# A gated graph layer on one Trainium2 core: table and result stores on ScalarE's queue, table copies on SyncE's

## The chip, the cores and the metric

The kernel runs on one core of a Trainium2 chip. Its time is the device time of a whole execution in microseconds (us). It is given as the median over several runs. A profiled execution is a run of its own: the profile's times are made against that run and not against the median.

The engines are TensorE (PE, matrix products; PEld is its weight load), VectorE (DVE), ScalarE (ACT), GpSimd (POOL) and SyncE (SP). SyncE computes nothing here: it only issues DMA transfers. ScalarE and GpSimd issue transfers as well, between their other instructions. A DMA that SyncE issues goes by queue q1, one that ScalarE issues by q10, and the gathers of GpSimd by q0. Each engine goes through its instructions in a fixed order.

## The reference

Sixteen batches of 1024 nodes with 256 values each, one adjacency matrix for all of them. About 0.8% of its entries, and its diagonal, are not zero.

```python
pre_u = einsum('bud,dk->buk', h, W1[:d])
pre_v = einsum('bvd,dk->bvk', h, W1[d:])
hidden = relu(pre_u[:, :, None, :] + pre_v[:, None, :, :] + b1)
S = sigmoid(einsum('buvk,ko->buvo', hidden, W2)[..., 0] + b2[0])
a = einsum('buv,bud->bvd', S * A, h)
m = einsum('uv,bud->bvd', A, h) * h
z = beta1 * h + beta2 * (a @ Wa + ba) + beta3 * (m @ Wm + bm)
```

So each target node v sums its neighbours' rows h_u twice: once scaled by the entry of A and a gate S of the edge, and once by the entry of A alone. The kernel computes the gate only for the edges that are there.

## The kernel before

**Tables.** The batches form 4 groups of 4. For each group g there is a table in HBM with one row of 8 KB per node: the first half holds pre_u of the four batches, the second half a copy of h of the four batches. A gather of 128 rows thus brings all that 128 edges need.

**Blocks and steps.** The loop runs over 32 blocks, each with one group and 128 targets. Targets 0 to 5 of groups 0 and 1 come first, then their targets 6 and 7, then groups 2 and 3. A block has 2 windows of 5 slots, so 10 steps of 128 edges, and there are 320 steps. In a step

- GpSimd gathers 128 table rows into one of 8 buffers (line 518),
- TensorE spreads pre_v of the targets over the edges (615) and VectorE adds it to the rows (647),
- VectorE takes relu times W2 and sums, four times, one for each batch (655),
- ScalarE takes the sigmoid (658) and scales the edges' one-hot columns by the gate (660, with 625 for the part without a gate),
- TensorE sums the rows of the slot into the targets (672).

At the end of a window half, ScalarE copies the sums out (680), TensorE transposes them (690), ScalarE copies those (693), and VectorE multiplies the m part by h (704). At the end of a block TensorE multiplies by Wa and Wm (721), ScalarE copies the product (726), and VectorE adds beta1 times h in the block's buffer h_blk (727).

**Work beside it.** Group 0's table is made ahead of the loop. The rows of the others are made inside it, piece by piece, where a script written out by hand puts them. For 128 nodes of a group: load_hT (434) brings the transposed h by SyncE; copy_h (439) copies h straight from the input in HBM into the table's second half; half_product (445) makes pre_u for two batches at a time; ScalarE copies it into one of two buffers, tab0 and tab1 (461), each of which exists once; and a store brings that to the table (465). Line 467 is the same store for rows made ahead of the loop, where one buffer holds all four batches.

h_blk has four buffers. It is loaded from the table at steps 5 and 7 of each block by SyncE (911) and stored to the output two steps after its product (729). The last block has its own load (917) and its own stores (767), shared by SyncE and ScalarE.

**What sets the order.** All of this is issued in a fixed order for each engine. `after(step, f)` puts a small action on a list for a later step, and `do(n)` runs the list of step n after that step's gate. The store of a tab buffer is put one step after its copy, and the store of h_blk two steps after its product. A DMA instruction whose data or buffer isn't ready holds everything behind it on the engine that issues it.

Of the kernel before, what the change touches and what calls it, by code (L numbers as in the profile page):

```python
# [13 lines left out]
P = 128  # L14
# [3 lines left out]
def kernel(  # L18
# [42 lines left out]
    nc = tc.nc  # L61
# [22 lines left out]
    table = [dram.tile([N, 2 * GD], FP, name=f"table{g}") for g in range(NG)]  # L84
# [135 lines left out]
    def small(name):  # L220
        return psm.tile([P, 512], FP, name="misc")
# [180 lines left out]
    def after(step, f):  # L402
        due.setdefault(step, []).append(f)
# [19 lines left out]
    def drop_hT(k):  # L423
        del hTs[k]
        if k in hT_of:
            hT_free.append(hT_of.pop(k))
# [7 lines left out]
        engine.dma_start(hTs[k].rearrange("p b c n -> p (b c) n"),  # L434
                         xT_rows[:, g * GB * DC:(g + 1) * GB * DC, nt * P:(nt + 1) * P])

    def copy_h(k, engine=nc.scalar):
        g, nt = k
        engine.dma_start(table[g][nt * P:(nt + 1) * P, GD:].rearrange("n (b d) -> n b d", b=GB),
                            x_rows[nt * P:(nt + 1) * P, g * GB:(g + 1) * GB, :])  # L440

    def half_product(p, hT, wt, h, begun):
        for bb in range(2):
            for i in range(DC):
                nc.tensor.matmul(p[:, bb * D:(bb + 1) * D], hT[:, 2 * h + bb, i, :], wt[:, i, :],  # L445
                                 start=(i == 0 and not begun), stop=(i == DC - 1), skip_group_check=begun)

    def add_row(p, parts):
        nc.tensor.matmul(p, unit, parts.unsqueeze(1).to_broadcast([P, 2, D]),  # L449
                         start=True, stop=False, skip_group_check=True)  # L450

    def rows(k, tab=None):

        g, nt = k
        for h in range(2):
            step = yield
            c = slice(2 * h * D, (2 * h + 2) * D)
            p = small("p")
            half_product(p, hTs[k], w_u, h, False)
            t = big.tile([P, 2 * D], FP, name=f"tab{h}", bufs=1) if tab is None else tab[:, c]  # L460
            nc.scalar.copy(t, p)
            if h == 1 and k in again:
                drop_hT(k)
            if tab is None:
                after(step + 1, lambda t=t, c=c: nc.sync.dma_start(table[g][nt * P:(nt + 1) * P, c], t))
        if tab is not None:
            after(step + 1, lambda: nc.sync.dma_start(table[g][nt * P:(nt + 1) * P, :GD], tab))

# [72 lines left out]
    for i in range(COPIES):  # L541
        copy_h(turn[i], nc.sync)
# [17 lines left out]
    for t, turns_ in enumerate(script):  # L560
        step = t - 100
        do(step)
        for c in turns_.split():
            if c == "r":
                if m % 2 == 0:
                    piece = rows(turn[m // 2], tabs[m // 2] if m // 2 < len(tabs) else None)
                    next(piece)
                go(piece, step)
                if m % 2 == 0 and m // 2 + COPIES < NT:
                    copy_h(turn[m // 2 + COPIES], nc.sync)  # L570
# [138 lines left out]
    def block_end(k):  # L709

        g, vt = order[k]
        hb = hbs[k]
        for h in range(2):
            for i, wt in ((1, w_a), (0, w_m)):
                step = yield
                if i:
                    pz = small("pz")
                    add_row(pz, bias_p)
                for bb in range(2):
                    for c in range(DC):  # L720
                        nc.tensor.matmul(pz[:, bb * D:(bb + 1) * D], LTs[k][:, 2 * h + bb, i if bb else 1 - i, c, :], wt[:, c, :],  # L721
                                         start=False, stop=(i == 0 and c == DC - 1), skip_group_check=True)
            z = pz.rearrange("p (b d) -> p b d", b=2)
            if step >= ROOM:
                z = LTs[k][:, 2 * h].rearrange("p k c n -> p (k c n)").rearrange("p (b d) -> p b d", b=2)
                nc.scalar.copy(z, pz.rearrange("p (b d) -> p b d", b=2))
            after(step + 1, lambda hb=hb[h], z=z: nc.vector.scalar_tensor_tensor(hb, hb, be1, z, ALU.mult, ALU.add))  # L727
            b = g * GB + 2 * h
            after(step + 2, lambda hb=hb[h], b=b: nc.sync.dma_start(
                out[b:b + 2, vt * P:(vt + 1) * P, :].rearrange("b p d -> p b d"), hb))  # L730
        del hbs[k], LTs[k]

# [59 lines left out]
    def made_rows(n):  # L792
        nonlocal piece, last
        if n in loads and loads[n] in turn[NT:NT + 2] and loads[n] not in begun:
            copy_h(loads[n])
            begun.add(loads[n])
        elif n in loads:
            if loads[n] in begun and loads[n][0] == 1:
                aside_.remove(loads[n])
            load_hT(loads[n])  # L800
            if loads[n] not in begun:
                copy_h(loads[n])
                begun.add(loads[n])
        if n in at:
            if at[n] != last:
                last = at[n]
                piece = rows(last)
                next(piece)
            go(piece, n)

    def products(n, k, s):
# [5 lines left out]
        if z <= s < z + 4 and 0 < k < BS:  # L817
            if s == z:
                end = block_end(k - 1)
                next(end)  # L820
            go(end, n)
# [50 lines left out]
    for n in range(total + 2):  # L872
        k, s = divmod(n, T)
# [32 lines left out]
        if s in (5, 7) and k < BS - 1:  # L906
            h = s // 7
            hb = big.tile([P, 2, D], FP, name="h_blk", bufs=4)
            hbs.setdefault(k, []).append(hb)
            g, vt = order[k]  # L910
# [31 lines left out]
    with tc.If(any_left > 0):  # L942
        with ExitStack() as s2:
# [4 lines left out]
            for vt in range(NT):  # L948
                hb = fb.tile([P, B, D], FP, name="fb_h")
# [100 lines left out]
```

## Time and profile before

| what | value |
|---|---|
| three runs | 1085.15, 1085.4, 1089.84 us; median 1085.4 |
| profiled execution, own time | 1098.79 us |
| its span in the profile | 1097.0 us |
| mean granted TensorE clock | 0.984 of full speed |
| GpSimd's gathers, line 518 | 320; q0 has 70.4% of the DMA time |
| q1 (SyncE) | 83776 packets, 78.66 MB, 22.5% of the DMA time |
| q10 (ScalarE) | 13296 packets, 13.11 MB, 3.5% |
| all DMA | 394.56 MB at a mean of 360 GB/s |
| DMAs issued in the loop by SyncE | h_blk loads 62, result stores 62, tab stores 48 |
| DMAs issued in the loop by ScalarE | copies of h 24 |

How to read it: a line such as "L465 SPq" names the kernel's line and the engine; the letter q after an engine means the engine's own issuing of DMAs and not its computing. "Busy" of an engine counts only its computing instructions. A wait "A <- B" says that A stood idle until B was done. A "remote" releaser is one that the profile could not name. The chain of waits is followed back from the last instruction. A row of slices gives, for a stretch of the span, how long each engine was busy in it.

### The profile page before, as it was taken

To read this page: it belongs to the slowest core of one execution; us is meant where nothing else is said; L and a number is where in the kernel's file an instruction comes from. 1 tells how busy PE (TensorE), PEld (TensorE's weight loads), DVE (VectorE), ACT (ScalarE), POOL (GpSimd) and SP (SyncE) were. 2 spreads that over 40 slices of the span, in tenths; PEclk is the share of its full clock that TensorE was granted. 3 is DMA by queue.
4 is the path that set the end of the run, shared out by engine and by line. 5 is a ranking of instruction groups with operands and counts; after the bars stand their busy time and mean duration, and the time that the engine had idled before them with its cause. 6 is when DMAs were issued, how large, how long until landed. Compare 5 with 4: busy or idle time off the path is not lost.

```text
span 1097.0 us, 24059 instructions
## 1 busy us (share of the span) xinstructions
PE 1027.7 (94%) x7645; PEld 730.7 (67%) x7645; DVE 1022.9 (93%) x3487; ACT 862.6 (79%) x2616; POOL 456.9 (42%) x456
## 2 busy tenths in 40 slices
PE   7777898999999999999999999999999999999986
PEld 6654676676666776667766777777766666666653
DVE  8686999898999999999998999999999999999994
ACT  3246787778888887798878888898889888888973
POOL 2665675455347334553332342333333333333330
PEclk9888999999999999999999999999999999999999
DMA  9989999999999999999999999999999999999991
GB/s 289 317 332 373 323 329 366 316 377 375 401 361 376 398 403 370 373 384 394 400 392 349 410 390 392 399 391 397 369 366 363 373 349 355 362 373 356 357 343 44
DMA packets 147752, 394.56 MB, mean 360 GB/s; under 512 B 18224, under 2 KB 94512, under 8 KB 111408
## 3 DMA queue, kind: packets, MB, share of 16 engines
q0 software_dynamic: 50544, 301.16, 70.4%
q1 hardware_dynamic: 83776, 78.66, 22.5%
q10 hardware_dynamic: 13296, 13.11, 3.5%
q8 instruction: 63, 1.03, 0.4%
q14 instruction: 73, 0.60, 0.1%
HBM read 396.93 MB, written 50.33 MB: 408 GB/s over the span
## 4 chain that ended last, share of the span: by engine, by line
PE 53%; DVE 26%; DMA 8%; issue 7%; ACT 4%; SPq 1%; POOL 1%; another core or an unknown queue 0%; ACTq 0%; POOLq 0%; DVEq 0%
PE misc L445 14%; PE acc L672 13%; DVE fetched L655 12%; PE misc L721 11%; DVE fetched L647 10%; PE pc L615 9%; PE misc L690 3%; DMA fetched<-table,uidx 2%; DMA table<-tab 2%; DMA out_dram<-h_blk 2%; PE misc L449 2%; DVE low L484 1%; ACT left L660 1%; DVE LT L704 1%; DVE h_blk L727 1%
## 5 line engine op out<-in xcount | busy, mean ns | idle before, releaser
L518 POOL DMA_INDIRECT fetched<-table,uidx x320 | 338.0, 1056 | 548.4 <-PE acc L672 412.9
L655 DVE SCALAR_TENSOR_TENSOR fetched<-fetched,w_b 128x256 f32<-128x256 f32 x1280 | 478.3, 420 | 0.0
L647 DVE TENSOR_TENSOR fetched<-fetched,pc 128x1024 f32<-128x1024 f32 x320 | 387.8, 1212 | 39.4 <-PE pc L615 25.9
L660 ACT ACTIVATE left<-left,gt 128x32 f32<-128x32 f32 (+1 forms) x1280 | 299.6, 305 | 10.4
L672 PE MATMUL acc<-fetched,left 128*32 128x256 f32 x4096 | 281.6, 385 | 12.0 <-issue 4.6
L615 PE MATMUL pc<-X,mark 128*128 128x512 f32 x640 | 244.7, 464 | 15.2 <-DVE fetched L647 14.8
L672 PEld LDWEIGHTS acc<-fetched,left 128*32 128x32 f32 x4096 | 128.7, 109 | 125.0 <-issue 38.0
L615 PEld LDWEIGHTS pc<-X,mark 128*128 128x128 f32 x640 | 106.0, 190 | 93.6 <-issue 40.4
L658 ACT ACTIVATE gt<-sc,b_b 128x4 f32<-128x4 f32 x320 | 95.9, 300 | 45.3 <-DVE fetched L655 40.1
L721 PE MATMUL misc<-w_m,LT 128*128 128x256 f32 x496 | 117.3, 379 | 0.0
L721 PE MATMUL misc<-w_a,LT 128*128 128x256 f32 x496 | 117.2, 379 | 0.0
L445 PE MATMUL misc<-w_v,hT 128*128 128x256 f32 x448 | 108.4, 386 | 0.0
L721 PEld LDWEIGHTS misc<-w_a,LT 128*128 128x128 f32 x496 | 93.8, 189 | 15.3 <-issue 0.4
L721 PEld LDWEIGHTS misc<-w_m,LT 128*128 128x128 f32 x496 | 93.8, 190 | 15.1
L625 ACT ACTIVATE left<-onehot,val 128x64 f32<-128x64 bf16 (+1 forms) x320 | 102.9, 322 | 0.0
L655 DVE DVE_READ_ACCUMULATOR fetched<-fetched,w_b 128x1 f32 x1280 | 101.0, 79 | 0.0
L385 POOL DMA_INDIRECT val<-in_adjT_dram,vidx x80 | 86.3, 1079 | 34.3 <-issue 20.7
L445 PEld LDWEIGHTS misc<-w_v,hT 128*128 128x128 f32 x448 | 87.0, 194 | 14.4
L690 PE MATMUL misc<-ident,ev 128*128 128x128 f32 x512 | 80.6, 281 | 17.1 <-ACT ev L680 6.1
L690 PEld LDWEIGHTS misc<-ident,ev 128*128 128x128 f32 x512 | 60.9, 142 | 45.5 <-ACT ev L680 16.2
L482 ACT CAST X<-misc 128x512 fp32r<-128x512 f32 x64 | 37.1, 579 | 59.3 <-PE misc L445 44.9
L693 ACT COPY LT<-misc 128x512 f32<-128x512 f32 x128 | 72.9, 570 | 11.9 <-PE misc L690 9.1
(181 smaller groups left out, 1011.4 us busy)
## 6 DMA issues: line engine op xcount, KB each, us to landing
h_blk<-table SPq DMA_DIRECT2D x62, 256.0 KB
out_dram<-h_blk SPq DMA_DIRECT2D x62, 256.0 KB
hT<-in_xT_dram SPq DMA_DIRECT2D x28, 512.0 KB
table<-in_x_dram ACTq DMA_DIRECT2D x24, 512.0 KB
table<-tab SPq DMA_DIRECT2D x48, 256.0 KB
fetched<-table,uidx POOLq DMA_INDIRECT x320
table<-in_x_dram SPq DMA_DIRECT2D x8, 512.0 KB
table<-fetched SPq DMA_DIRECT2D x8, 512.0 KB
```

Source lines behind the costliest of these rows:

```text
L385: nc.gpsimd.indirect_dma_start(out=val[:, i, j:j + 1], out_offset=None, in_=adj_flat, in_offset=bass.IndirectOffsetOnAxis(ap=vidx[:, i, j: ...
L445: nc.tensor.matmul(p[:, bb * D:(bb + 1) * D], hT[:, 2 * h + bb, i, :], wt[:, i, :], start=(i == 0 and not begun), stop=(i == DC - 1), skip ...
L518: nc.gpsimd.indirect_dma_start(out=fetched[at_slot[n]], out_offset=None, in_=table[g], in_offset=bass.IndirectOffsetOnAxis(ap=uidx[:, vt * ...
L615: nc.tensor.matmul(pcs[n][:, c], marks[n // TW][:, j * P:(j + 1) * P], cuts[k][:, w, c], start=True, stop=True)
L625: nc.scalar.activation(lefts[n][:, :m, 1::GB, :], onehot[:, i, o:o + m, :].unsqueeze(2).to_broadcast([P, m, GB // 2, V]), AF.Copy, scale=v ...
L647: nc.vector.tensor_tensor(t, t, pcs.pop(n), ALU.add)
L655: nc.vector.scalar_tensor_tensor(t[:, b, :], t[:, b, :], 0.0, w2_b, ALU.max, ALU.mult, accum_out=sc[:, b:b + 1])
L658: nc.scalar.activation(gt, sc, AF.Sigmoid, bias=b2_b)
L660: nc.scalar.activation(lefts[n][:, :m, 2 * b, :], lefts[n][:, :m, 1 + b // 2 * GB, :], AF.Copy, scale=gt[:, b:b + 1])
L672: nc.tensor.matmul(accs[h][b * 2 * V:(b + 1) * 2 * V, r, :], left[:, i, 2 * b - b % 2:2 * b - b % 2 + 2].rearrange("p k v -> p (k v)"), f[ ...
L690: nc.tensor.transpose(pt[:, r, :, c, :], ev[:, r, c * P:(c + 1) * P], ident)
L721: nc.tensor.matmul(pz[:, bb * D:(bb + 1) * D], LTs[k][:, 2 * h + bb, i if bb else 1 - i, c, :], wt[:, c, :], start=False, stop=(i == 0 and ...
```

## The change

Three calls change their engine; nothing else does.

```diff
-    def copy_h(k, engine=nc.scalar):
+    def copy_h(k, engine=nc.sync):
         g, nt = k
         engine.dma_start(table[g][nt * P:(nt + 1) * P, GD:].rearrange("n (b d) -> n b d", b=GB),
                             x_rows[nt * P:(nt + 1) * P, g * GB:(g + 1) * GB, :])
...
             if tab is None:
-                after(step + 1, lambda t=t, c=c: nc.sync.dma_start(table[g][nt * P:(nt + 1) * P, c], t))
+                after(step + 1, lambda t=t, c=c: nc.scalar.dma_start(table[g][nt * P:(nt + 1) * P, c], t))
...
-            after(step + 2, lambda hb=hb[h], b=b: nc.sync.dma_start(
+            after(step + 2, lambda hb=hb[h], b=b: nc.scalar.dma_start(
                 out[b:b + 2, vt * P:(vt + 1) * P, :].rearrange("b p d -> p b d"), hb))
```

In the loop the 48 tab stores and the 62 result stores are issued by ScalarE instead of SyncE, and the 24 copies of h by SyncE instead of ScalarE. The stores of line 467, the copies ahead of the loop and the last block's own loads and stores stay where they were. The computing instructions of TensorE, VectorE and GpSimd keep their order. ScalarE's list has 1820 rows instead of 1734, which is 110 stores more and 24 copies fewer.

## The prediction

> **What bounds the kernel now.** I read the page from the top: busy shares, the chain that ended last, then the middle of the run in slices of 30 us, then the waits.
>
> ```profile
> PE 1027.7 (94%) x7645; PEld 730.7 (67%) x7645; DVE 1022.9 (93%) x3487; ACT 862.6 (79%) x2616; POOL 456.9 (42%) x456
> ...
> PE 53%; DVE 26%; DMA 8%; issue 7%; ACT 4%; SPq 1%; POOL 1%; another core or an unknown queue 0%; ACTq 0%; POOLq 0%; DVEq 0%
> ```
>
> The first line is busy time, the second the chain. TensorE and VectorE share the bound; ScalarE has 1097.0 − 862.6 = 234 us to spare, 0.73 us in each of the 320 steps. Who bounds where is seen in the slices:
>
> ```profile
> core 0: us, PE busy (x) PEld busy (x) DVE busy (x) ACT busy (x) POOL busy (x), PEclk, DMA share, GB/s
> 510.00:540.00 30.00, 29.93 (x233) 21.78 (x232) 28.76 (x98) 26.20 (x81) 10.49 (x10) 1.00 1.02 396
> 570.00:600.00 30.00, 25.77 (x197) 18.20 (x196) 23.98 (x78) 21.02 (x70) 8.84 (x8) 0.94 0.97 353
> ...
> 180.00:210.00 30.00, 24.50 (x166) 17.06 (x165) 24.01 (x87) 17.83 (x56) 15.81 (x15) 0.94 0.96 319
> ...
> 150.00:180.00 30.00, 29.65 (x226) 21.96 (x219) 29.96 (x104) 25.79 (x80) 18.89 (x20) 1.00 1.02 383
> 900.00:930.00 30.00, 28.79 (x223) 19.99 (x222) 30.00 (x103) 26.84 (x81) 11.25 (x11) 1.00 0.96 355
> 90.00:120.00 30.00, 22.98 (x133) 14.87 (x135) 21.73 (x74) 17.00 (x54) 20.53 (x20) 0.89 0.99 360
> ```
>
> In the middle (510) TensorE never rests; late (900) VectorE never rests. Three slices stand out, in which both rest: 90, 180 and 570. Only such holes can be won by a change that touches queues, unless it makes new ones. What they wait for:
>
> ```profile
> ACT tab L461 <- remote: 10.6, 2, 7.8
> ACT tab L461 <- DMA table<-tab: 5.0, 1, 5.0
> PE misc L690 <- ACT tab L461: 4.4, 2, 3.7
> SPq L729 <- DVE h_blk L727: 418.8, 41, 23.0
> SPq L911 <- DMA out_dram<-h_blk: 21.7, 4, 13.7
> ```
>
> The columns are the total wait, how often, and the longest. ScalarE's copy into the table buffer (line 461) waits three times, at 104, 184 and 577 us. The 577 wait is explained in the SyncE queue's timeline:
>
> ```profile
> 540.48 13.77 SPq L911 DMA_DIRECT2D h_blk<-table  x1
> 554.34 0.40 SPq L729 DMA_DIRECT2D out_dram<-h_blk  x1
> 554.95 5.91 SPq L465 DMA_DIRECT2D table<-tab  x2
> ...
> 565.61 12.33 SPq L729 DMA_DIRECT2D out_dram<-h_blk  x1
> ```
>
> Start and duration lead each line. The buffers were filled by 552, but the stores (465) left only at 554.95, behind a load (911) that held SyncE for 13.77 us; the chain runs through this store for 21.77 us. The next block's copy at 576.80 stood 5.01 us for it, and TensorE's transposes (690) 3.74 us for the copy.
>
> **What the Trainium skill says.** "DMA: Bandwidth & Descriptors", section "Issuing engines are not separate DMA queues": whichever engine starts them, transfers run on the same 16 DMA engines, and several issuers save only sequencer time. The trace agrees as far as it goes: the DMA share is near 1.0 at 360 GB/s whatever queue is busy. Same page, "Queues, rings and completion order": each queue has a ring per DMA engine, served in turn by packet, so a store on the other queue needn't wait behind SyncE's packets. Landings here and below are the last packet of a DMA on its queue in the trace, counted from the issue. Stores not behind an hT load (1024 packets) landed about 4 us after issue (104.92 to 108.9), the mean of tab stores is 7.3 and the worst 16.6 us. "Perfetto Trace Analysis", section "DMA Instruction — HWDGE (DVE, Sync)": an issue's reported time includes waiting for the shared descriptor generator, but not the data movement. The trace fits: 0.33 to 0.56 us normally, up to 13.77 when held.
>
> **The change, part by part.**
>
> *1. The stores leave SyncE.* SyncE loses 48 tab stores and 62 result stores, and with them the waits for VectorE's line 727 (418.8 us of 41 waits). Its other DMAs (hT at 434, h_blk at 911) issue as soon as their buffers are free. The 577 stall is caused by a store kept behind a load; on ScalarE's queue it leaves within a step or two of its copy, more than 20 us ahead of the next. Worth: 29.93 − 25.77 = 4.2 us of TensorE. At 184 the copy waited 2.85 us while SyncE's tab store, issued about 180.3, had stood behind a result store: taken at 2.9 us. Together 7.1 us. Next late there is TensorE itself, as at 510. At 104 SyncE's store was issued at its usual time and other engines waited "remote" too; I take nothing for that one.
>
> *2. ScalarE issues them.* Added: 48 × 0.333 + 62 × 0.388 = 40.0 us of sequencer time; removed: the copies of h, 24 × 0.56 = 13.4; net 26.6 us and 86 instructions. The copies show what such an issue costs ScalarE now. The four scalings (660) with a copy inside and without:
>
> ```profile
> 499.71 0.91 ACT L660 ACTIVATE left<-left,gt 128x16 f32<-128x16 f32 x4
> ...
> 503.34 0.31 ACT L660 ACTIVATE left<-left,gt 128x16 f32<-128x16 f32 x1
> 503.43 0.56 ACTq L439 DMA_DIRECT2D table<-in_x_dram  x1
> 503.55 0.69 ACT L660 ACTIVATE left<-left,gt 128x16 f32<-128x16 f32 x3
> ```
>
> From 503.34 to 504.24 is 0.90 us, against 0.91: the issue ran beside work already queued. Bounds: 0 if always hidden, 26.6 if never; I take 0.6, since 234 us of idle time absorb most of what isn't hidden, and ScalarE is on 4% of the chain.
>
> *3. ScalarE's stores wait, and ScalarE with them.* Behind a waiting store stand the sigmoid (658), the gate scalings, the transposes' copies (693), and for these TensorE. Three kinds:
> - For their data. The tab copy is ScalarE's own. For a result store VectorE's 727 stands in its order ahead of the sums (655) whose sigmoid ScalarE has already used. Nothing new.
> - For a completion semaphore. In the program's listing each DMA of the two queues takes one of eight in turn, and first waits until the DMA eight before has landed. 116 of ScalarE's DMAs wait so, 51 of them for one of SyncE's. Setting the issue times of the new order against the landings of before (hT mean 15.5, worst 39.0 us; h_blk 10.3 and 23.3), about a dozen have under 3 us in hand, and four have landed too late in the loop, by 4.8, 3.1, 1.1 and 1.0: 10 us in all. ScalarE's slack at 577 was 5.01 − 3.74 = 1.3 us. Less 1.3 where that covers it: 3.5 + 1.8 = 5.3. But SyncE, no longer behind 727, issues its loads earlier: lower bound 0, upper 10, value 1.5.
> - For a tab buffer. Where the next tab copy follows after only four steps (about 156 and 232 us), ScalarE reaches the store after the next step's gate, some 3 to 6 us later than an unheld SyncE did, and the landing (about 4 us) may come after the next copy: 0 to 4 us twice, value 1.5.
>
> *4. The copies of h go to SyncE's queue.* 24 × 512 packets of 1 KB. Their rows are gathered a group later, so later landing (12.4 us mean now) costs nothing. They lie ahead of hT loads: an hT lands later by up to 12 us, but is loaded a block (about 30 us) ahead. SyncE is off the path: 0, bounds 0 to 4.
>
> *Sum*, against the profiled execution of 1098.8 (span 1097.0 and 1.8 around it): −7.1 + 0.6 + 1.5 + 1.5 = −3.5, so 1095.3. That execution is 13.4 over the median of the runs; the same step gives 1085.4 − 3.5 = 1081.9, said as 1082. Its own range is 1077 (all of 7.1 and a little of the holes at 90 to 200) to 1087.
>
> **Rivals.** A measurement of this kernel can tell about 0.5%, 5.4 us, from no change.
>
> *B, faster: all early holes close.* If the holes at 90 and 180 are also due to SyncE's order, VectorE gains 29.96 − 21.73 = 8.2 and 29.96 − 24.01 = 6.0, with 4.2 at 577: 18.4. 1085.4 − 18.4 + 2.1 for the new waits = about 1069. For it: all three have the same waiting line 461. Against: at 104 the store was not late, and several engines stood.
>
> *C, slower: ScalarE is held at its own stores.* On SyncE eight of these single stores were held for 2.4 to 13.8 us, 54.6 us in all (5.38, 13.76, 2.39, 4.85, 7.52, 5.79, 12.33, 2.56 in its timeline), which cost nothing there. On ScalarE a hold beyond 1.3 us stops the gate, and then TensorE. If a quarter follows them, 13.7: 1081.9 + 13.7 = 1096. It decides once the DMA eight before, or the ring, is still busy when ScalarE arrives. For it: 51 semaphores come from SyncE's large loads, now with copies in their queue. Against: not one of 24 copies was held on ScalarE (longest 0.70), one of them at 533.49, inside a held SyncE load of 531.85 to 534.34.
>
> *D, nothing moves.* The 16 DMA engines are full on either queue, and the 577 hole reappears elsewhere: 1085.
>
> **How the numbers follow.** Forecast 0.43, B 0.16, C 0.33, D 0.08. Faster by over 0.5% (below 1080.0): 0.10 of the forecast's and all of B, 0.26. Within: 0.32 of the forecast's, D, and 0.04 of C, 0.44. Slower (over 1090.8): 0.01 and 0.29 of C, 0.30. The range 1068 to 1102 takes in B's and C's centres, and leaves out some 0.07 below and 0.10 above. The likeliest alone: 1077 to 1087.
>
> **What would show it.** Right: no wait of line 461 on the table store at 577; that slice near 29.9 us of TensorE; SyncE's wait of 418.8 for line 727 gone; line 660 beside issues unchanged. Step 3 wrong: ScalarE idle ahead of 465 or 729, with issues of several us in its queue, and TensorE waiting for lines 660 or 693. Step 1 too small: the 90 and 180 slices full (B). Step 4 wrong: TensorE's 445 waiting for an hT.

## The result, and the profile after

The changed kernel takes 1119.4 us (median of six executions, 1113.5 to 1128.9) where the kernel before takes 1085.7 (1083.3 to 1089.8). The ratio is 1.0296, with a 95% interval of 1.0255 to 1.0337: 2.6 to 3.4% slower. The forecast was 1082, its range 1068 to 1102. The rival C had the right sign and about the right place, with 1096.

The profiled execution of the changed kernel took 1113.5 us, with a span of 1111.7. First its page, busy shares and chain:

```profile
PE 1027.3 (92%) x7645; PEld 732.0 (66%) x7645; DVE 1022.7 (92%) x3487; ACT 863.0 (78%) x2616; POOL 459.5 (41%) x456
...
PE 41%; DVE 24%; DMA 15%; ACT 12%; issue 6%; another core or an unknown queue 1%; ACTq 1%; SPq 0%; POOL 0%; DVEq 0%; POOLq 0%
```

TensorE, VectorE and ScalarE are as busy as before within 0.4 us, GpSimd within 2.6. The work is the same, so in this pair of executions the loss is waiting. On the chain DMA has risen from 8% to 15% and ScalarE from 4% to 12%. The slices show where. First the kernel before in two stretches that the prediction does not show, then the changed kernel:

```profile
core 0: us, PE busy (x) PEld busy (x) DVE busy (x) ACT busy (x) POOL busy (x), PEclk, DMA share, GB/s
240.00:270.00 30.00, 28.57 (x199) 19.85 (x192) 26.91 (x88) 24.75 (x75) 21.23 (x19) 1.00 1.02 377
390.00:420.00 30.00, 28.01 (x221) 19.76 (x221) 30.00 (x115) 24.22 (x74) 9.20 (x9) 1.00 1.02 389
```

```profile
150.00:180.00 30.00, 25.54 (x169) 18.93 (x166) 25.75 (x90) 20.37 (x62) 15.56 (x17) 0.94 1.00 356
240.00:270.00 30.00, 23.69 (x150) 17.00 (x151) 19.10 (x59) 18.44 (x56) 15.30 (x16) 0.89 0.77 265
390.00:420.00 30.00, 26.10 (x195) 18.68 (x195) 27.33 (x104) 22.50 (x69) 8.30 (x9) 0.94 0.95 364
570.00:600.00 30.00, 29.93 (x232) 21.65 (x224) 28.78 (x96) 25.23 (x78) 10.56 (x10) 1.00 1.02 392
```

The hole at 570 is gone, as forecast. New ones have come at 150, 240 and 390, in which both TensorE and VectorE rest. The waits of SyncE, and then those of ScalarE, name their makers (total, times, longest):

```profile
SPq L911 <- DMA out_dram<-h_blk: 528.4, 46, 28.3
```

```profile
ACT tab L461 <- DMA table<-tab: 17.1, 3, 7.6
ACT tab L461 <- remote: 11.0, 1, 11.0
...
ACT LT L693 <- DMA table<-in_x_dram: 5.8, 1, 5.8
```

SyncE's 418.8 us of waiting for line 727 are gone as forecast. It now runs ahead and stands at its h_blk loads (911) until a result store has freed the buffer, which costs nothing in itself. ScalarE's waits for table stores and at line 693 are new. (The "remote" wait of 11.0 has its like in the kernel before, 10.6 in two, and ends with an update of TensorE's semaphore.) Two kinds of waits make the loss.

**One: the table buffer.** ScalarE's timeline around the hole at 240, its DMA issues and copies into the table buffers alone:

```profile
228.65 0.59 ACT L461 COPY tab<-misc 128x512 f32<-128x512 f32 x1 [2.17 <-PE misc L445]
...
230.01 0.40 ACTq L729 DMA_DIRECT2D out_dram<-h_blk  x1
...
230.44 0.71 ACTq L465 DMA_DIRECT2D table<-tab  x1
...
232.01 0.34 ACTq L465 DMA_DIRECT2D table<-tab  x1
...
244.22 0.58 ACT L461 COPY tab<-misc 128x512 f32<-128x512 f32 x1 [7.55 <-DMA table<-tab]
```

The two tab stores left right behind a result store, on the same queue. In the packets of that queue the first tab store began only 5.8 us after its issue. A transfer has landed for the program when the last update of its completion semaphore comes; in the trace that was 13.7 and 15.2 us after the two issues. The next copy, four steps later, stood 7.55 us and began at 244.22, 0.08 us after the first of them had landed. The same happened at 163.03 us (6.84) and 200.67 (2.72).

TensorE pays for such a stall twice. Its timeline at the same place, ahead of the stall and behind it:

```profile
234.43 1.89 PE L445 MATMUL misc<-w_u,hT__2105 128*128 128x256 f32 x8
...
244.86 0.80 PE L449 MATMUL misc<-b_p,unit 128*128 128x512 f32 x1 [6.01 <-ACT tab L461]
245.45 3.62 PE L445 MATMUL misc<-w_v,hT 128*128 128x256 f32 x8
```

Eight products of one shape take 3.62 us behind the stall and 1.89 before it. From 243 to 249 us the granted TensorE clock was 0.50. It was so too for some 3 us behind each of the stalls at 163.03, 200.67 and 405.36.

**Two: a DMA eight back.** ScalarE's and SyncE's timelines at the hole at 390:

```profile
405.36 0.40 ACTq L729 DMA_DIRECT2D out_dram<-h_blk  x1
405.80 0.48 ACTq L465 DMA_DIRECT2D table<-tab  x1
406.32 0.58 ACT L693 COPY LT<-misc 128x512 f32<-128x512 f32 x1 [5.83 <-DMA table<-in_x_dram]
```

```profile
368.37 0.39 SPq L434 DMA_DIRECT2D hT<-in_xT_dram  x1
368.81 3.16 SPq L439 DMA_DIRECT2D table<-in_x_dram  x1
```

Line 693 copies transposes and needs no DMA. What it stood behind is the result store of 405.36. In the program's listing the eighth DMA before that store, whose completion semaphore it takes over, is the copy of h that SyncE issued at 368.81. This copy's last packet landed at 404.69, behind an hT load on the same queue. The store left 0.67 us later, and ScalarE's gate and TensorE's products behind it. The trace bears the listing out: both instructions use the same one of eight semaphores, the copy's last update of it came at 405.34, and the store left 0.02 us after that. Four stores of ScalarE in the loop left 0.02 to 0.08 us after such an update, with 8.7 us in all of idle ScalarE ahead of its next computation; every other had over 1.6 us in hand. In the kernel before no DMA of ScalarE in the loop left like that.

### The profile page after: what moved, and what is told of

It is laid out like the page before. It is cut to its first block, busy times and chain, and to the rows that moved or that the text cites. A ratio compares the mean times of both kernels' runs of the same rounds, so it can differ in the third digit from the quotient of the medians.

```text
span 1111.7 us, 24027 instructions
## 1 busy us (share of the span) xinstructions
PE 1027.3 (92%) x7645; PEld 732.0 (66%) x7645; DVE 1022.7 (92%) x3487; ACT 863.0 (78%) x2616; POOL 459.5 (41%) x456
## 4 chain that ended last, share of the span: by engine, by line
PE 41%; DVE 24%; DMA 15%; ACT 12%; issue 6%; another core or an unknown queue 1%; ACTq 1%; SPq 0%; POOL 0%; DVEq 0%; POOLq 0%
PE misc L445 12%; DVE fetched L655 11%; PE acc L672 10%; DVE fetched L647 9%; PE misc L721 9%; PE pc L615 6%; DMA table<-in_x_dram 6%; DMA table<-tab 3%; ACT left L660 3%; DMA fetched<-table,uidx 2%; PE misc L690 2%; ACT X L489 2%; DMA h_blk<-table 2%; PE misc L449 1%; ACT LT L726 1%
## 5 line engine op out<-in xcount | busy, mean ns | idle before, releaser
L647 DVE TENSOR_TENSOR fetched<-fetched,pc 128x1024 f32<-128x1024 f32 x320 | 388.1, 1213 | 38.8 <-PE pc L615 21.9
L672 PE MATMUL acc<-fetched,left 128*32 128x256 f32 x4096 | 277.5, 385 | 6.4 <-issue 2.2
L615 PE MATMUL pc<-X,mark 128*128 128x512 f32 x640 | 245.1, 464 | 14.7 <-DVE fetched L647 12.7
L445 PE MATMUL misc<-w_u,hT 128*128 128x256 f32 x320 | 78.3, 393 | 7.3 <-issue 3.7
```

Of the source, the lines that this page charges most:

```text
L615: nc.tensor.matmul(pcs[n][:, c], marks[n // TW][:, j * P:(j + 1) * P], cuts[k][:, w, c], start=True, stop=True)
L647: nc.vector.tensor_tensor(t, t, pcs.pop(n), ALU.add)
L672: nc.tensor.matmul(accs[h][b * 2 * V:(b + 1) * 2 * V, r, :], left[:, i, 2 * b - b % 2:2 * b - b % 2 + 2].rearrange("p k v -> p (k v)"), f[ ...
```

## Experiments

The times are ratios to the kernel before on the same chip, with 95% intervals. "Buffer theory" and "semaphore theory" are the two kinds above; "issue theory" is the rival that ScalarE's additional issue time is the loss.

**A second execution of each kernel** (no edit), run last, but needed first.

> The kernel before, one more profiled execution. If the stall of 5.0 us at step 148 belongs to the kernel it is there again; if it was of that execution alone, line 461 has no wait for the table store there, and the span is nearer 1084.

> The changed kernel, one more profiled execution. Buffer theory: jumps of the lag at steps 22, 32 and 42 again, of 4 to 8 us each. Semaphore theory: again jumps after step 80, at the stores that have a copy or an hT load eight back (steps 90, 112 to 115, 130, 210), though not all of the same size.

The kernel before made 1.0002 (0.9982 to 1.0023), with a span of 1085.1. The stall at 577 us is not there:

```profile
570.00:600.00 30.00, 29.90 (x233) 21.72 (x232) 28.81 (x95) 26.27 (x82) 10.54 (x11) 1.00 1.02 405
```

So the prediction's gain was a property of one execution, the one that lay 13.4 us above the median. The changed kernel made 1.0276 (1.0232 to 1.0320), span 1117.9, with its waits in the same places:

```profile
ACT tab L461 <- DMA table<-tab: 18.0, 3, 7.7
ACT LT L693 <- DMA table<-in_x_dram: 11.2, 2, 5.6
```

These two executions give the account of the loss. The lag is the start of a step's sigmoid (line 658) in one trace less its start in the second trace of before, in us. Each row is one execution, and the traces come from several chips, on which the kernel before had medians of 1082 to 1092 us; the first trace of before itself gains 4.7 us from step 18 to 51 and 5.8 after it. So differences of some 5 us in this table say nothing:

| kernel | step 18 | step 51 | step 160 | step 319 |
|---|---|---|---|---|
| change, second execution | 0.5 | 22.5 | 29.1 | 33.8 |
| change, first execution | 1.1 | 21.9 | 26.3 | 28.5 |
| both stores, copies with ScalarE | −0.7 | 17.0 | 29.0 | 37.3 |
| change, third table buffer | −3.9 | −5.9 | 7.9 | 12.6 |
| change, tab store at once | −2.6 | −5.2 | 6.4 | 11.6 |
| before, third table buffer | −5.7 | −9.2 | −5.2 | −5.4 |
| tab stores alone | 4.4 | 4.5 | 10.2 | 9.8 |

In the second execution of the change the lag jumps by 5.0 at step 22, 5.6 at 32 and 33, 7.8 at 42 and 3.1 at 47, which is the stage in which table buffers are used again after four steps; then by 4.8 at step 90 and 5.7 at 210, where a store of ScalarE meets a copy eight back. From step 18 to 51 it gains 22.0, and after that 11.3. The waits alone are 18.0 us for the table stores, and 11.2 of idle ScalarE at stores that left at once after a DMA eight back had landed. TensorE was busy for 1032.4 us, 14.8 more than in the second execution of before, at a mean granted clock of 0.974 against 0.992: part of the loss is the slower products behind the stalls. How much of the lag is that, the runs don't separate.

**The parts alone, and in pairs.** Each is the diff of the change with only the lines named.

> Only the 48 tab stores of line 465 go to ScalarE's queue; result stores stay with SyncE, copies of h with ScalarE. Buffer theory (a tab store leaves later and lands slower from ScalarE, so the next copy into the single buffer waits): nearly all of the loss, 17 to 20 us, and line 461 waiting on the table store near steps 22, 32 and 42. Semaphore theory (ScalarE's stores stand until SyncE's DMA eight back has landed): 0 to 4 us, since 62 of its 110 stores are gone and the copies are off SyncE. Issue theory (sequencer time of the issues): 48 x 0.333 = at most 16 us, spread over steps 0 to 200 evenly and not in jumps.

> Only the 62 result stores of line 729 go to ScalarE's queue. Buffer theory: no loss, rather a gain of up to 5 us, as tab stores no longer stand behind a result store in SyncE's order. Semaphore theory: 2 to 8 us slower, in jumps where a result store of ScalarE meets an hT load eight back. Issue theory: at most 62 x 0.388 = 24 us, evenly over the loop.

> Only the 24 copies of h go to SyncE's queue; all stores stay with SyncE, so ScalarE issues no DMA in the loop but the last block's. Buffer theory: 0 to 4 us slower, where a tab store lands behind 512 packets more on the same queue. Semaphore theory: no loss, as nothing on ScalarE waits for a DMA's landing. Issue theory: up to 13 us faster.

> Both kinds of stores go to ScalarE's queue, the copies of h stay with ScalarE: the change without its third part. Buffer theory: as the change, but for what the copies did to it, 17 to 22 us slower than before. Semaphore theory: the waits of the change at 405, 469 and 778 us were for copies of h that landed 18 to 36 us after their issue on SyncE's queue, so without them it is some 8 to 12 us faster than the change. Issue theory: 13 us slower than the change.

> The change without its tab stores: result stores go to ScalarE, copies of h to SyncE, tab stores stay with SyncE. Each of the two alone made 0.1 to 0.2%. If the loss lies in the parts meeting (ScalarE's stores waiting for copies and hT loads eight back): 4 to 8 us slower than before. If it needs the tab stores on ScalarE: within 3 us of before.

> The change without its result stores: tab stores to ScalarE, copies of h to SyncE. Tab stores alone made 1.05%, copies alone 0.1%. Buffer theory: 1 to 1.5%. If the copies add semaphore waits of the tab stores (nine of them have a copy eight back): 1.5 to 2.5%.

| moved | ratio | interval |
|---|---|---|
| tab stores (465) | 1.0105 | 1.0053 to 1.0156 |
| result stores (729) | 1.0017 | 0.9988 to 1.0046 |
| copies of h (439) | 1.0011 | 0.9986 to 1.0037 |
| both stores | 1.0172 | 1.0108 to 1.0237 |
| result stores and copies | 1.0041 | 1.0022 to 1.0060 |
| tab stores and copies | 1.0059 | 1.0037 to 1.0081 |
| all three (the change) | 1.0296 | 1.0255 to 1.0337 |

The parts alone sum to 1.3%, all three make 3.0%. So more than half of the loss lies in their meeting. The issue theory falls: the 62 result stores are more than half of ScalarE's new issues and cost nothing that can be measured. The buffer theory as stated (tab stores alone make it, 17 to 20 us) falls too. Alone they gain no lag from step 18 to 51 (4.4 to 4.5), while with the result stores beside them they gain 17.7. It takes a result store ahead of the tab store on one queue. What makes the 1.05% of the tab stores alone is not shown: the trace, of the fastest of four executions, has 2.0 us of waits for table stores and one of 2.3 us of the second kind. The semaphore theory's 8 to 12 us between both stores and the change agree with the 1.2% measured, of which the intervals allow 0.5 to 2.0; the run of both stores rests on three executions of 1108.7 to 1125.2 us. But the second kind of wait isn't gone without the copies: an hT load took their place in this wait of line 693, and the lag after step 51 was 20.3 us in the traced execution, the slowest of the three.

```profile
ACT LT L693 <- DMA hT__6824<-in_xT_dram: 7.0, 1, 7.0
```

Result stores with copies met the 4 to 8 us expected of their meeting in size (0.41%), but not in kind: in the trace no store of ScalarE but one of the last block, with 0.3 us, stood for a DMA eight back. The lag came from step 18 to 51 (9.1), with TensorE and ScalarE waiting for each other; what began that is not shown. Tab stores with copies, at 0.59%, stayed below both expectations: the copies added nothing to the tab stores that the intervals can tell.

**A third table buffer**, in the changed kernel and, as a control, in the kernel before.

```diff
-            t = big.tile([P, 2 * D], FP, name=f"tab{h}", bufs=1) if tab is None else tab[:, c]
+            t = big.tile([P, 2 * D], FP, name="tab", bufs=3) if tab is None else tab[:, c]
...
-        lefts[n] = wk.tile([P, 2, 2 * GB - 1, V], FP, name="left", bufs=5)
+        lefts[n] = wk.tile([P, 2, 2 * GB - 1, V], FP, name="left", bufs=4)
```

> The changed kernel with three table buffers in turn instead of two fixed ones, so a buffer is used again after nine steps or more instead of four. (To make room, the buffers of line 624 go from five to four, and two of the list stage's from two to one.) Buffer theory: line 461's waits of 6.8, 2.7 and 7.6 us go, and with them the lag's jumps at steps 22, 32 and 42, so 15 to 19 us faster than the change, near 1103. Semaphore theory: as the change, within 3 us.

> The kernel before with the same three table buffers and the same smaller ones: what the buffers alone do. Buffer theory: 0 to 5 us faster than before, the wait at 577 us gone; slower only if the smaller buffers cost something, which would then have to be taken off the run with the changed kernel. Semaphore theory: the same.

The changed kernel made 1.0190 (1.0135 to 1.0245), the kernel before 1.0008 (0.9987 to 1.0029). Line 461's waits on the table store are gone from the first, and with them the lag from step 18 to 51: −2.0 instead of +22.0. The first kind is shown, in its place. But only 1.1% of time came back, not the 17 us and more that went there: the lag from step 51 on grew from 11.3 to 18.5. The second kind took its place: eleven stores left within 0.08 us of the landing eight back, with 29.6 us of idle ScalarE in all, where each execution of the change had four, with 8.7 and 11.2. One stall of it, first ScalarE and then SyncE:

```profile
515.33 0.40 ACTq L729 DMA_DIRECT2D out_dram<-h_blk  x1
515.76 0.60 ACTq L465 DMA_DIRECT2D table<-tab  x1
516.41 0.59 ACT L693 COPY LT<-misc 128x512 f32<-128x512 f32 x1 [10.81 <-issue]
```

```profile
479.57 0.43 SPq L434 DMA_DIRECT2D hT<-in_xT_dram  x1
480.05 15.50 SPq L439 DMA_DIRECT2D table<-in_x_dram  x1
```

The copy of h behind the hT load took 15.50 us to issue and landed at 514.56. It is the eighth DMA before the store of 515.33, which left 0.77 us later.

**The tab store at once**, in the changed kernel, with a single buffer of each kind as before.

```diff
-                after(step + 1, lambda t=t, c=c: nc.scalar.dma_start(table[g][nt * P:(nt + 1) * P, c], t))
+                nc.scalar.dma_start(table[g][nt * P:(nt + 1) * P, c], t)
```

> The changed kernel with ScalarE's tab store right after its copy instead of a step later. Buffer theory: the store leaves 3 to 5 us earlier, so the waits of 6.8, 2.7 and 7.6 shrink to 2 to 4, 0 and 3 to 4: 8 to 13 us faster than the change. Semaphore theory: the stores meet the DMA eight back earlier, so as the change or up to 5 us slower. Against both: ScalarE stands for its own copy of 0.58 us 48 times, at most 28 us slower if nothing hides it.

It made 1.0184 (1.0133 to 1.0235), 12 us better than the change: the tab stores leave ahead of the result store, and no wait of line 461 on a table store is left. Tab stores landed after 7.6 us in the mean, against 10.1 in the change. ScalarE's standing for its own copies doesn't show. The second kind stays:

```profile
ACT LT L693 <- DMA table<-in_x_dram: 12.2, 2, 6.6
```

**Result stores three steps later**, in the changed kernel.

```diff
-            after(step + 2, lambda hb=hb[h], b=b: nc.scalar.dma_start(
+            after(step + 5, lambda hb=hb[h], b=b: nc.scalar.dma_start(
```

> The changed kernel with ScalarE's result stores three steps (about 9 us) later, so that SyncE's DMA eight back has landed when ScalarE comes to them. Semaphore theory: the waits at 405, 533 and 594 us go, and the lag's jumps at steps 90 and 130: 6 to 9 us faster than the change. Buffer theory: little, 0 to 4 us faster, as the tab stores at 149, 190 and 230 us no longer leave right behind a result store on the same queue.

It made 1.0260 (1.0208 to 1.0312), no different from the change within the intervals. The trace shows why, and it speaks for both kinds. Three steps later a result store no longer leaves ahead of the tab stores that matter: one wait of line 461 for a table store is left, of 0.5 us, and the lag from step 18 to 51 is −0.8. The semaphore theory's 6 to 9 us did not come, because a store that is put elsewhere in the order follows another DMA eight back. After step 51 the lag grows by 30.4, and ScalarE's long waits are again of the second kind:

```profile
ACT X L486 <- DMA hT<-in_xT_dram: 13.5, 2, 11.0
ACT X L482 <- DMA hT<-in_xT_dram: 12.2, 1, 12.2
ACT X L482 <- DMA h_blk<-table: 9.9, 1, 9.9
```

They don't stand for the data of TensorE's products. ScalarE's timeline at the longest, then SyncE's:

```profile
299.13 0.38 ACTq L729 DMA_DIRECT2D out_dram<-h_blk  x1
299.55 0.58 ACT L482 CAST X<-misc 128x512 fp32r<-128x512 f32 x1 [12.17 <-DMA hT<-in_xT_dram]
```

```profile
262.62 8.14 SPq L434 DMA_DIRECT2D hT<-in_xT_dram  x1
```

The product that line 482 copies was done by 287.6. The hT load of 262.62 had the store's semaphore; it landed at 299.11, and the store left 0.02 us later. TensorE's sums (672) stood 10.2 us for ScalarE.

**Which transfer eight back.** Both stores on ScalarE with three table buffers, but the copies of h left with ScalarE; and tab stores alone with three buffers.

> Both stores on ScalarE with three table buffers, the copies of h left with ScalarE. With the copies on SyncE it was 1.9%. If the copies on SyncE make the semaphore waits: 0.3 to 0.8%. If hT loads make as many in their place: near 1.9%, with ScalarE's stores leaving 0.4 to 0.9 us after an hT load eight back has landed.

> Only the tab stores on ScalarE's queue, now with three table buffers in turn (and the same smaller buffers as in the runs with a third one). Buffer theory: the 1.05% of the tab stores alone shrinks to 0 to 0.4%. If the semaphores (two hT loads eight back, at about 579 and 758 us) make it: it stays near 1%.

Both stores made 1.0091 (1.0059 to 1.0124), against 1.0190 with the copies on SyncE, so the copies account for about half of what is left, and the hT loads may for the rest: two stores left 0.59 and 0.73 us after the last packet of an hT load eight back (0.02 and 0.08 after its semaphore's last update), with 8.0 us of idle ScalarE. Tab stores alone made 1.0054 (1.0022 to 1.0087); whether the third buffer helped them (1.0105 without) the intervals don't tell.

**Long transfers off the shared semaphores.** The loop's hT loads and copies of h go by GpSimd, which in the trace uses eight semaphores of its own. The first kernel is before with three table buffers; the second has both stores on ScalarE besides.

```diff
-            load_hT(loads[n])
+            load_hT(loads[n], nc.gpsimd)
...
-                copy_h(loads[n])
+                copy_h(loads[n], nc.gpsimd)
```

> A control: the kernel before with three table buffers, and with the hT loads and copies of h of the loop issued by GpSimd, which doesn't share the eight completion semaphores of ScalarE and SyncE. 30 us of issue (some 50 at about 0.6 to 1 us) on an engine with 58% idle time: 0 to 15 us slower than before, by no theory in question.

> The same with both stores on ScalarE: the changed kernel with three table buffers and hT loads and copies issued by GpSimd, so that no hT load and no copy is ever the DMA eight back of a store of ScalarE. Against the control, semaphore theory: within 4 us (0.4%), where with these transfers on SyncE's queue the stores on ScalarE cost 1.8% with three buffers. Issue theory: still 1.8%, about 20 us.

They made 1.0119 (1.0061 to 1.0177) and 1.0167 (1.0122 to 1.0212). The stores on ScalarE now cost 1.0167 / 1.0119 = 1.0047, uncertain by 0.7%, where with the long transfers on SyncE they cost 1.0190 / 1.0008 = 1.0182, uncertain by 0.6%. In the second kernel's trace one store of ScalarE, in the last block, left at once after a DMA eight back had landed, with 0.1 us of idle; all others had over 5 us in hand, and no wait of line 693 names a DMA. ScalarE issues the same 110 stores here and in the changed kernel with a third buffer, so neither their issue nor their data is the cost: it is the wait for the transfers eight back. The second kind is shown, with the reserve that the expected 4 us lies inside the interval and so does more, and that the control is itself 1.2% slower than before, which may hide a small stall. No kernel tried was faster than before.

## Why the prediction was wrong, step by step

*Step 1, the gain of 7.1 us:* wrong in its base. The mechanism at 577 was real in its trace, and gone in the changed kernel's. But a second execution of the kernel before hasn't this stall either, and takes the median's time. The stall was part of the 13.4 us by which that execution lay above the median; I made the sum against the former and carried it over to the latter. The 2.9 us at 184 were a misreading: that copy's wait ended with an update of TensorE's semaphore at 184.47, and the store of the buffer it writes had landed at 170.8.

*Step 2, the issues' 26.6 us taken at 0.6:* right. The result stores alone cost 0.17% (−0.12 to 0.46), and in the changed kernel the issues kept to medians of 0.40 us (729) and 0.35 (465).

*Step 3, completion semaphores, value 1.5 of 0 to 10:* right mechanism, wrong size: 8.7 and 11.2 us of idle ScalarE at the stores in the two executions (lag after step 51: 6.6 and 11.3). My own count, four late landings and 10 us, was near it; the fault was to take 1.5 of it. The margins were taken from landings of before, where copies landed 12.4 us after issue, and those of SyncE's queue were read too early: by the semaphores hT loads took 19.8 us in the mean, not 15.5. I let an earlier SyncE shorten the waits. It didn't: from SyncE's queue the copies landed after 21.8 us on average, 42.1 at worst.

*Step 3, table buffers, value 1.5 of 0 to 8:* the failing term. The waits measured 17.1 and 18.0 us, and the lag from step 18 to 51 grew by 20.8 and 22.0. I named two of the places; 32 was a third, and 12 is the fourth such reuse. The later issue was as forecast (149.64 against 145.25 us for step 18's store), but "landing about 4 us" was not: behind a result store on ScalarE's queue it was 10 to 15. The readings themselves were too low as well: the semaphores' updates give 10.1 us in the mean and 26.3 at worst for the tab stores of before (I had 7.3 and 16.6), and the mean of the changed kernel is 10.1 too. So stores didn't land later in general; those that are needed after four steps did (step 18's: 5.0 us before, 13.3 after). That stores leave SyncE's queue only to queue behind each other was not in the sum. The Trainium skill ("DMA: Bandwidth & Descriptors", section "Queues, rings and completion order") says that each queue has a ring per DMA engine, and what I drew from it, a store that needn't wait behind SyncE's packets, left out the packets of ScalarE itself. The trace agrees with the page, with the first packet 5.8 us after issue.

*Step 4, the copies of h at 0:* right that no gather waited for them in a way that shows (one line of the profile puts a gather behind a copy for 8.9 us, but the semaphore that released it was a table store's, and TensorE stood 0.45 us at most around it), wrong that they cost nothing in the change. Alone they do (1.0011); with ScalarE's stores they are what the stores wait for, about 1% with a third buffer.

*The sum:* −7.1 was about 0, the two 1.5 were 8.7 to 11.2 and 17.1 to 18.0, and the slower products behind each stall were in no term.

*The rivals:* B fell. All early holes did not close. C had the side, and named the point that decides, a DMA eight back that is still busy, but took its price from SyncE's held issues (eight of them; a ninth, of 4.78 us at 554.95, lay hidden in a merged line), which were not what held ScalarE: its own issues stayed under 1.3 us. The sentence against C, that no copy was ever held on ScalarE, was true of copies that ran apart from SyncE's pace.

## What to carry to other kernels

An engine that computes and issues DMAs stops computing at every DMA that may not go yet, and that includes the wait for a completion semaphore to come free, so count which transfer each of its DMAs follows on that semaphore and how late it lands in the new order. Moving a store in the order changes which transfer that is. A store moved to a quieter queue is only early if nothing of its own lies ahead of it there: look at what leaves in the same step, and when the buffer is needed again. A stall in a profiled execution that is over 1% above the median may be that execution's own; take a second one before booking it as a gain.

## What the runs showed of the hardware that I had not expected

The same copy of 512 packets landed, by its completion semaphore, 12.7 us after issue on average from ScalarE's queue (24 copies, before), 19.5 from SyncE's with the stores still there (22 copies), and 21.0 from SyncE's with the stores gone from it (22 copies). Taking 110 stores off SyncE's queue did not make it the quicker one for the copies, which SyncE issues right behind an hT load of 1024 packets. The issue itself is part of it: 0.57 us on average on ScalarE, 2.4 and 2.0 on SyncE, 3.16 and 15.50 us in the two lines of SyncE above.

A store that had stood for a shared semaphore left 0.02 to 0.08 us after its last update. And a stall of TensorE of about 6 us cost more than its length: the products behind it took 3.62 us instead of 1.89. In the second execution of before the granted clock was whole from 72 to 1081 us; in the changed kernel's it was halved nine times in that stretch, for 3.4 to 6.8 us each.

The Trainium skill's remark that several issuing engines only save sequencer time ("DMA: Bandwidth & Descriptors", section "Issuing engines are not separate DMA queues") holds here in that the change gained nothing, but moving an issuer was not neutral: it cost 3.0%.
